# Group statistics on VectorE, the bias of v in its own rows, halved output banks, and the first image's raw weights in other tiles

## The chip, the core and the metric

The kernel runs on one core of a Trainium2 chip, on fp32 data throughout. The metric is the device time of one execution in microseconds. PE is the matmul engine, PEld its weight load, DVE the vector engine, ACT the scalar engine, POOL GpSimd, SP the engine that only issues DMAs.

## What is computed

An attention block over 16 images of 512 channels and 32 x 32 positions:

```python
xg = x.reshape(b, NUM_GROUPS, -1)                      # 8 groups of 64 channels
mu = jnp.mean(xg, axis=-1, keepdims=True)
var = jnp.var(xg, axis=-1, keepdims=True)
xn = ((xg - mu) * jax.lax.rsqrt(var + EPS)).reshape(b, c, h, w)
xn = xn * norm_gamma[:, None, None] + norm_beta[:, None, None]
qkv = jnp.einsum('oc,bchw->bohw', qkv_w, xn) + qkv_b[:, None, None]
q, k, v = jnp.split(qkv, 3, axis=1)                    # 4 heads of 128 channels
attn = jax.nn.softmax(jnp.einsum('bhnd,bhmd->bhnm', q, k) * scale, axis=-1)
out = jnp.einsum('bhnm,bhmd->bhnd', attn, v)
...
out = jnp.einsum('oc,bchw->bohw', proj_w, out) + proj_b[:, None, None]
return x + out
```

## The kernel before

Channels lie on the 128 partitions: an image is four tiles `x` of 128 x 1024 (`load_x`). The attention of an image goes head by head; a head has 8 blocks of 128 keys, and a *step* is one block. In each step, for each half of 512 queries, `scores` makes one 128x512 matmul into a bank `s` (L844), ACT takes its exp into `p` (L850), and `weighted_sum` adds the block before to the output bank `po` (L912). `po` is one tile of two banks, one half of the queries in each, with a single buffer; after the last block ACT copies each half to `o` (L919). On DVE, `tot` sums the exps (L856, L858; the additions are kept in `added[b, h, j]`), `denominators` transposes and reduces that sum, `spread_inverse` sends the reciprocals through DRAM to all partitions, and `divide` multiplies `o` (L922) four blocks into the next head.

The projections (q and k, for each pair of heads; v; the output projection `proj`) use Strassen's seven products on two levels, in `two_levels` and `strassen`. The outer level has four groups of products (`OUTER`); each makes seven inner products of 256 columns (L604) in banks `x` and `y`. ACT copies some to SBUF (`u`, L484), and DVE adds the others to results `R` in three tiles `r0`, `r1`, `r2` (L628, tag `r{g % 3}`, one buffer each). `combine` adds the groups (L677), and `finish` makes the final rows: for q and k one scalar_tensor_tensor with the bias (L712); for v an addition into a tile `vt` (L766), a transpose by 32 x 32 blocks into `vu` (L769), a DMA to DRAM (L777) and back as `v` (L782). `vt`, `vu`, the staged weights of site v and proj in the first image, and the residual `y` of the output projection share the four buffers of `ypool`.

These projection units lie between the steps. `plan_head` gives each of a head's 8 blocks a list of units: head 0 takes the second pair's q and k, head 1 the projection of the image before, head 2 the first pair's q and k of the next image, head 3 the v of the next image. Where an instruction of a unit stands on its engine is set by a scheduler at build time, by priorities (`tc.high_priority(URGENT)`) and by order edges (`tc.issue_after(ins)`: behind `ins` on its engine).

In head 1 the next image is also normalised. `stats_chunk` makes, on ACT, the mean and variance of each channel of a chunk. `stats_group` brings them together over the 64 channels of a group, in three parts that are tied to `added[b - 1, 1, n]`: `Norm.group_steps` multiplies the four columns of means by the averaging matrix `avg` on PE (`pm`, L83), takes the deviations on DVE (L82 to L87), multiplies again (`pv`, L88), adds EPS (L89), and POOL raises to the power -0.5 (L90). `scale` and `shift` make the factors (L76, L100, L102), and `normalise` applies them to halves of chunks, on ACT (L109) or, in image 0 for even chunks, on DVE (L112). `x_sums` then makes Strassen's sums of x.

The first image has more to do. There weights are loaded raw (`stage_blocks`, L355, on SP's queue), summed (`stage_sums`, L387 and L388), turned into factors (`group_weights`, L415 to L439) and kept in DRAM (L441, `kept_v`, `kept_proj`), whence later images load them (L406). `kept_group` does this for v in blocks 0 and 1 of head 1, for proj in blocks 3 to 6, after `stage_blocks("proj")` in block 2. `bias_of_v` multiplies proj's staged weights by the bias of v, one column each, on PE (`pb`, L935), and adds the product to proj's bias, so that v's bias need not be added anywhere else.

The last image's projection (`last_projection`, L999) is written out by hand. `general_path` is not taken with these inputs.

Of the kernel before, what the change touches and what calls it, by code (L numbers as in the profile page):

```python
# [10 lines left out]
F32 = mybir.dt.float32  # L11
# [175 lines left out]
def fast_path(ctx, tc, x, sources, out, consts, flag, dims):  # L187
# [35 lines left out]
    ones = one.tile([BLK, 1], F32, name="ones")  # L223
    xs, xb, vs, qs, ks, os_, ob = {}, {}, {}, {}, {}, {}, {}
# [23 lines left out]
    nc.vector.memset(neghalf, -0.5)  # L248
    for t, src in (
        (gamma_sb, gamma), (beta_sb, beta), (qkb_sb, qk_b), (vb_sb, v_b), (projb_sb, proj_b)  # L250
    ):
        nc.gpsimd.dma_start(t, src)
# [3 lines left out]
    def stats_chunk(b, c):  # L256
        if c == 0:
            mvs[b] = gn.tile([P, NCC, 2], F32, tag="mv", name=f"mv_{b}")

        junk = lpool.tile([P, N], F32, tag="tt", name=f"junk_{b}_{c}")  # L260
        sums = gn.tile([P, 3], F32, tag="st", name=f"sums_{b}_{c}")
        nc.scalar.activation(junk, xs[b, c], AF.Identity, accum_out=sums[:, 0:1])
        nc.scalar.mul(mvs[b][:, c, 0:1], sums[:, 0:1], 1.0 / N)
        nc.scalar.mul(sums[:, 1:2], sums[:, 0:1], -1.0 / N)
        nc.scalar.activation(
            junk, xs[b, c], AF.Square, bias=sums[:, 1:2], accum_out=sums[:, 2:3]
        )
        nc.scalar.mul(mvs[b][:, c, 1:2], sums[:, 2:3], 1.0 / N)

    def stats_group(b):  # L270


        g = []

        def part(n, first, last):
            if not g:
                g.extend(norm.group_steps(mvs[b]))
            with tc.issue_after(added[b - 1, 1, n].ins), tc.high_priority(URGENT):
                for step in g[first:last]:
                    step()  # L280

        def scale():
            n = 4 if b > 1 else 3
            part(n, 9, 10)
            with tc.issue_after(added[b - 1, 1, n].ins), tc.high_priority(URGENT):
                mu, sc = norm.result
                sh = norm.shift(mu, sc)
            for c in range(NCC):
                scaled[b, c] = sc, sh, c

        return [lambda: part(2, 0, 6), lambda: part(3, 6, 9), scale]
# [75 lines left out]
    def stage_blocks(site):  # L367
# [4 lines left out]
        if site in ("proj", "v"):  # L372
# [381 lines left out]
    def v_groups(b):  # L754
# [3 lines left out]
        def finish(which, h, a, c):  # L758
            pair, half = int(which[1]) - 1, int(which[2]) - 1
            if (b, pair) not in vs:  # L760
# [4 lines left out]
            t = ypool.tile([P, HALF], F32, tag="y", name=f"vt_{b}_{pair}_{h}_{half}")  # L765
            nc.vector.tensor_add(t, a, c)  # L766
# [4 lines left out]
                t.rearrange("p (j q i) -> p j q i", q=n, i=BLK),  # L771
# [135 lines left out]
    def weighted_sum(s, half):  # L907
        b, h, j = where(s)
        if j == 0 and half == 0:
            po[b, h] = ps_o.tile([P, N], F32, tag="o", name=f"po_{b}_{h}")  # L910
        i = ts(half, HALF)
        nc.tensor.matmul(  # L912
            po[b, h][:, i], v_block(b, h, j), ps[s][:, i],
            start=(j == 0), stop=(j == NB - 1),
        )
        if j == NB - 1:
            if (b, h) not in os_:
                os_[b, h] = opool.tile([P, N], F32, tag="o", name=f"o_{b}_{h}")
            last_eviction[b] = nc.scalar.copy(os_[b, h][:, i], po[b, h][:, i])  # L919

    def divide(b, h):
        nc.vector.tensor_mul(os_[b, h], os_[b, h], rinv.pop((b, h)))  # L922

# [4 lines left out]

    def bias_of_v(o):

        acc = ps_a.tile([P, HALF], F32, tag="y", name=f"pb_{o}")
        half, r = divmod(o, 2)
        for c in range(NCC):
            block = stage["proj"][f"a{half + 1}{c // KC + 1}"]
            nc.tensor.matmul(  # L935
                acc[:, 0:1], block[:, ts(r * KC + c % KC, P)], vb_sb[:, c : c + 1],
                start=(c == 0), stop=(c == NCC - 1),
            )
        nc.vector.tensor_add(
            projb_sb[:, o : o + 1], projb_sb[:, o : o + 1], acc[:, 0:1]  # L940
        )
# [116 lines left out]

    def plan_head(b, h):
# [9 lines left out]
        elif h == 1:  # L1069
# [4 lines left out]
            else:  # L1074
                plan[0].append(lambda: load_x(b + 1))
                spread(plan, [lambda c=c: stats_chunk(b + 1, c) for c in range(NCC)], 2, 4)
                sums, power, scale = stats_group(b + 1)
                if b == 0:

                    plan[4] += [sums, power, scale]  # L1080
                else:
                    plan[4].insert(0, sums)
                    plan[4].insert((len(plan[4]) + 1) // 2, power)
                    plan[5].insert(0, scale)
                for r in range(2):
                    plan[5 + r] += [

                        lambda c=c, half=half: normalise(b + 1, c, half, b > 0 or c % 2 == 1)
                        for c in range(KC * r, KC * r + KC) for half in range(NH2)
                    ]  # L1090
                plan[6].append(lambda: x_sums(b + 1, (1,)))
            if b == 0:
                for g in range(len(OUTER)):
                    plan[g // 2].append(lambda g=g: kept_group("v", g))
                    plan[NB // 2 - 1 + g].append(lambda g=g: kept_group("proj", g))
                plan[2].append(lambda: stage_blocks("proj"))
                spread(plan, [lambda o=o: bias_of_v(o) for o in range(NCC)], 3, 5)
# [111 lines left out]

    plan = []  # L1210
    for s in range(steps + 1):
# [12 lines left out]
        for half in range(NH2):  # L1224
            if s < steps:
# [4 lines left out]
                if half == 1 and j == 4 and s > NB:  # L1230

                    with tc.issue_after(added[b, h, 4].ins):
                        divide(*where(s - NB)[:2])
            if s > 0:
# [12 lines left out]
def general_path(ctx, tc, x, sources, out, consts, dims):  # L1247
# [26 lines left out]
    with tc.For_i(0, B, 1) as b:  # L1274
# [16 lines left out]
        for h in range(HEADS):  # L1291
# [9 lines left out]
            for qb in range(NB):  # L1301
# [27 lines left out]
                nc.scalar.copy(o[h][:, ts(qb, P)], acc[:, :P])  # L1329
# [46 lines left out]
```

## Time and profile before

| | |
|---|---|
| time, median of 3 runs | 3169.58 us (3167.83 to 3171.18) |
| the profiled execution | 3171.08 us, of which the span 3169.3 |
| granted TensorE clock | 1.00 throughout |
| busy: PE, DVE, ACT, POOL | 3156.8, 2635.8, 1438.3, 516.3 us |
| one image in the middle (pv to pv) | 195.8 us |
| L83 pm, 128x4, and L88 pv, 128x4 | 30 passes each, mean 214 and 263 ns |
| L935 pb, 128x1 | 32 passes, mean 245 ns |
| L766 vt, L769 vu, L712 qk (DVE) | 711, 1131, 744 ns |
| L109 normalise, L985 bias of 128x1024 (ACT) | about 0.81 and 1.14 us |

An fp32 matmul is two passes, each with its own weight load, and the profile counts passes. A line of the timeline is: start in us, length in us, engine, source line, operation, output<-inputs, shape, how many in a row, and in brackets the idle time before it and what ended it. Matmuls overlap, so the length of a pass is more than its distance to the next start. A line of the waits is: who <- waited for whom: us in total, times, longest.

### The profile page before, as it was taken

Reading aid. Unit: us, or ns where it says so; the run is one execution under the profiler, and the core shown is the slowest. Engines: PE = TensorE matmul, PEld = TensorE weight load, DVE = VectorE, ACT = ScalarE, POOL = GpSimd, SP = SyncE. Lnnn points to the kernel's source line nnn. Section 1 sums busy time; section 2 is a strip of 40 time slices with the busy share of each in tenths; the row PEclk is TensorE's granted clock in tenths of the full one; section 3 lists DMA queues with packets and bytes.
Section 4 is the critical chain, followed back from the end, with each engine's and each line's share of the span. In section 5 each row is a group of like instructions: output and inputs, shape, how many; then the busy total and the mean of one; then the engine's idle time right before and its main releaser. Section 6 shows DMA issues by size and latency. Waiting matters only on the chain.

```text
span 3169.3 us, 34227 instructions
## 1 busy us (share of the span) xinstructions
PE 3156.8 (100%) x10502; PEld 2188.2 (69%) x10502; DVE 2635.8 (83%) x4642; ACT 1438.3 (45%) x2711; POOL 516.3 (16%) x896
## 2 busy tenths in 40 slices
PE   9999999999999999999999999999999999999999
PEld 7566676677776776767767667677676776766664
DVE  9878879788897888878888787987879978788785
ACT  3535435354353443535435454453534545344333
POOL 0011221111211112211122111222012221122200
PEclk9999999999999999999999999999999999999999
DMA  5554554545545555454554545555455564555531
GB/s 176 186 190 154 187 173 152 173 152 194 168 164 163 155 184 176 167 165 144 193 173 159 170 144 192 167 174 171 144 177 170 176 187 133 178 158 187 180 119 48
DMA packets 210668, 524.83 MB, mean 166 GB/s; under 512 B 32176, under 2 KB 65456, under 8 KB 210480
## 3 DMA queue, kind: packets, MB, share of 16 engines
q1 hardware_dynamic: 133088, 282.39, 28.6%
q0 software_dynamic: 64000, 204.54, 19.3%
q10 hardware_dynamic: 13392, 35.66, 3.5%
q8 instruction: 86, 1.41, 0.2%
q14 instruction: 102, 0.84, 0.1%
HBM read 389.30 MB, written 133.17 MB: 165 GB/s over the span
## 4 chain that ended last, share of the span: by engine, by line
PE 96%; DVE 2%; DMA 1%; issue 0%; SPq 0%; POOL 0%; ACT 0%; ACTq 0%; DVEq 0%
PE s L844 27%; PE po L912 27%; PE qk_x L604 12%; PE qk_y L604 9%; PE pp_x L604 6%; PE v_x L604 6%; PE v_y L604 4%; PE pp_y L604 4%; PE lx L999 0%; DVE qk_t L572 0%; DMA x<-in_x 0%; PE ly L999 0%; DVE tot L858 0%; DVE qk_r L628 0%; DVE qk L712 0%
## 5 line engine op out<-in xcount | busy, mean ns | idle before, releaser
L912 PE MATMUL po<-p,v 128*128 128x512 f32 x2048 | 1049.4, 594 | 0.7 <-ACT p L850 0.7
L850 ACT ACTIVATE p<-s 128x512 f32<-128x512 f32 x1024 | 610.6, 596 | 963.7 <-PE s L844 960.0
L844 PE MATMUL s<-qk,qk 128*128 128x512 f32 x2048 | 1047.4, 593 | 0.3 <-DVE qk L712 0.3
L912 PEld LDWEIGHTS po<-p,v 128*128 128x128 f32 x2048 | 603.6, 302 | 322.7 <-issue 214.5
L858 DVE TENSOR_TENSOR tot<-tot,p 128x1024 f32<-128x1024 f32 x385 | 470.2, 1221 | 158.1 <-ACT p L850 156.1
L844 PEld LDWEIGHTS s<-qk,qk 128*128 128x128 f32 x2048 | 387.7, 190 | 88.6 <-issue 29.9
L604 PEld LDWEIGHTS qk_x<-qk_t,w 128*128 128x128 f32 x1344 | 251.8, 190 | 166.1 <-issue 75.3
L604 PE MATMUL qk_x<-qk_t,w 128*128 128x256 f32 x1344 | 356.3, 382 | 0.1
L484 ACT COPY qk_u<-qk_x 128x512 f32<-128x512 f32 (+1 forms) x256 | 136.2, 532 | 229.6 <-PE qk_x L604 229.6
L777 POOL DMA_DIRECT2D vd<-vu x120 | 66.6, 556 | 902.9 <-DVE vu L769 899.5
L628 DVE TENSOR_TENSOR qk_r<-qk_y,qk_u 128x512 f32<-128x512 f32 (+1 forms) x256 | 158.1, 618 | 34.7 <-ACT qk_u L484 21.5
L578 POOL DMA_DIRECT2D kept_t<-qk_t x240 | 129.3, 540 | 278.5 <-DVE qk_t L572 212.0
L604 PEld LDWEIGHTS pp_x<-pp_t,w_proj 128*128 128x128 f32 x630 | 117.2, 190 | 74.7 <-issue 32.3
L628 DVE TENSOR_TENSOR v_r<-v_y,v_u 128x512 f32<-128x512 f32 (+1 forms) x120 | 76.6, 638 | 110.5 <-ACT v_u L484 80.3
L604 PE MATMUL pp_x<-pp_t,w_proj 128*128 128x256 f32 x630 | 167.8, 383 | 0.0
L782 POOL DMA_DIRECT2D v<-vd x240 | 140.5, 592 | 166.6 <-DMA vd<-vu 63.3
L604 PE MATMUL v_x<-v_t,w_v 128*128 128x256 f32 x630 | 166.6, 381 | 0.0
L828 POOL DMA_DIRECT2D out_y<-y x120 | 65.9, 550 | 603.3 <-DVE y L827 601.5
L604 PEld LDWEIGHTS v_x<-v_t,w_v 128*128 128x128 f32 x630 | 118.4, 190 | 55.3 <-issue 19.1
L604 PE MATMUL qk_y<-x,w 128*128 128x256 f32 x512 | 142.2, 379 | 1.5 <-DVE qk_r L628 1.5
L769 DVE STREAM_TRANSPOSE vu<-vt 128x512 f32<-128x512 f32 x120 | 135.7, 1131 | 4.5 <-DMA vd<-vu 4.4
L712 DVE SCALAR_TENSOR_TENSOR qk<-qk_r,qkb_sb,qk_r 128x512 f32<-128x512 f32 x192 | 137.7, 744 | 1.6
(203 smaller groups left out, 4420.0 us busy)
## 6 DMA issues: line engine op xcount, KB each, us to landing
w<-kept SPq DMA_DIRECT2D x90, 512.0 KB, 3.7
kept_t<-qk_t POOLq DMA_DIRECT2D x180, 256.0 KB, 3.5
v_t<-kept_t SPq DMA_DIRECT2D x180, 256.0 KB, 2.9
w<-kept SPq DMA_DIRECT2D x90, 384.0 KB, 3.3
rinv<-row ACTq DMA_DIRECT2D x63, 512.0 KB, 5.0
x<-in_x POOLq DMA_DIRECT2D x60, 512.0 KB, 4.6
vd<-vu POOLq DMA_DIRECT2D x120, 256.0 KB, 3.0
v<-vd POOLq DMA_DIRECT2D x240, 128.0 KB, 4.2
```

The source lines that it names most:

```text
L484: nc.scalar.copy(t[n][:, :width], t["x"][:, :width])
L578: nc.gpsimd.dma_start(t, to)
L604: nc.tensor.matmul(acc[:, ts(i, Q)], have["w"][t][:, i, slot, :], inner(i, bn), start=(first and i == 0), stop=True, skip_group_check=True,)
L628: nc.vector.tensor_add(dst, view(a), view(c))
L712: nc.vector.scalar_tensor_tensor(st[b, h][:, ts(half, HALF)], a, qkb_sb[:, i : i + 1], c, ALU.add, ALU.add)
L769: nc.vector.transpose(u.rearrange("p (q i j) -> p j q i", q=n, i=BLK), t.rearrange("p (j q i) -> p j q i", q=n, i=BLK),)
L777: nc.gpsimd.dma_start(rows[which][ts(h, P), :], u)
L782: nc.gpsimd.dma_start(vs[b, pair][ts(q, BLK), half].rearrange("m h (k i) j -> m (h k) (i j)", k=n), rows[which].rearrange("(k m) (q e) -> ...
L844: nc.tensor.matmul(sc, ks[b, h][:, ts(j, P)], qs[b, h][:, ts(half, HALF)], start=True, stop=True)
L850: exps[s] = nc.scalar.activation(ps[s][:, ts(half, HALF)], sc, AF.Exp, scale=SCALE)
L858: added[b, h, j] = nc.vector.tensor_add(tot[b, h][:, i], tot[b, h][:, i], ps[s][:, i])
L912: nc.tensor.matmul(po[b, h][:, i], v_block(b, h, j), ps[s][:, i], start=(j == 0), stop=(j == NB - 1),)
```

## The change

The group statistics of images 1 to 15 move from PE to DVE: `stats_chunk` writes mean and sum of squares into a `table` of 128 x 2 x 32, zero but for four columns. `gather` transposes it by 32 x 32 blocks, copies each quadrant's rows to its neighbour, and aggregates 64 triples (count, mean, sum of squares) with bn_aggr; `scale` transposes the result back. It is tied to `added[b - 1, 1, 3]`, the scaling as before. `bn_aggr`'s input is in the tile of tag `tt`.

The bias of v is added in v's `finish`, in place in the tile of the result (`c`), so that `vt` goes; in image 0 it is added to `o` by ACT after the division, in blocks 2 of heads 2 and 3 and of image 1's head 0, and in block 6 of the latter. The 16 matmuls `pb` go.

`po` becomes two tiles of one bank each. In the first image proj's raw weights are staged in `r0` and `r1`, at the start of block 0 of head 1, and `kept_group("proj")` runs in blocks 2 to 5. Image 1 is normalised there one chunk at a time: the even chunks in blocks 5 and 6 on DVE, the odd ones a block later on ACT, each instruction behind an exp.

```diff
+    table = one.tile([P, 2, BLK], F32, name="table")
...
+    nc.gpsimd.memset(table, 0.0)
...
     def stats_chunk(b, c):
-        if c == 0:
-            mvs[b] = gn.tile([P, NCC, 2], F32, tag="mv", name=f"mv_{b}")
-
+        mean, spread_ = (
+            (mvs[b][:, c, 0:1], mvs[b][:, c, 1:2]) if b == 0
+            else (table[:, 0, c : c + 1], table[:, 1, c : c + 1])
+        )
...
-        nc.scalar.mul(mvs[b][:, c, 0:1], sums[:, 0:1], 1.0 / N)
+        nc.scalar.mul(mean, sums[:, 0:1], 1.0 / N)
...
-            junk, xs[b, c], AF.Square, bias=sums[:, 1:2], accum_out=sums[:, 2:3]
+            junk, xs[b, c], AF.Square, bias=sums[:, 1:2],
+            accum_out=sums[:, 2:3] if b == 0 else spread_,
         )
-        nc.scalar.mul(mvs[b][:, c, 1:2], sums[:, 2:3], 1.0 / N)
+        if b == 0:
+            nc.scalar.mul(spread_, sums[:, 2:3], 1.0 / N)
 
     def stats_group(b):
-        g = []
-
-        def part(n, first, last):
-            if not g:
-                g.extend(norm.group_steps(mvs[b]))
-            with tc.issue_after(added[b - 1, 1, n].ins), tc.high_priority(URGENT):
-                for step in g[first:last]:
-                    step()
+        v = nc.vector
+        quads = P // BLK
+        k = slice(0, NCC)
+        t = {}
+
+        def gather():
+            t["all"] = lpool.tile([P, N], F32, tag="tt", name=f"groups_{b}")
+            rows = t["all"][:, : 6 * BLK].rearrange("p (s j) -> p s j", s=3)
+            both = t["both"] = t["all"][:, 6 * BLK : 6 * BLK + 2]
+            ve = t["all"][:, 6 * BLK + 2 : 6 * BLK + 3]
+            v.memset(rows[:, 0, :], float(N))
+            v.transpose(rows[:, 1:3, :BLK], table)
+            for q in range(quads):
+                v.tensor_copy(rows[ts(q, BLK), 1:3, BLK:], rows[ts(q ^ 1, BLK), 1:3, :BLK])
+            v.bn_aggr(both, rows.rearrange("p s j -> p j s"))
+            v.tensor_scalar_add(ve, both[:, 1:2], EPS)
+            nc.gpsimd.tensor_tensor(both[:, 1:2], ve, neghalf[:, 0:1], ALU.pow)
 
         def scale():
-            n = 4 if b > 1 else 3
-            part(n, 9, 10)
-            with tc.issue_after(added[b - 1, 1, n].ins), tc.high_priority(URGENT):
-                mu, sc = norm.result
-                sh = norm.shift(mu, sc)
+            back = t["all"][:, 8 * BLK : 10 * BLK].rearrange("p (s j) -> p s j", s=2)
+            v.transpose(back, t["both"].unsqueeze(2).to_broadcast([P, 2, BLK]))
+            sc = gn.tile([P, NCC], F32, tag="sc", name="sc")
+            v.tensor_mul(sc, back[:, 1, k], gamma_sb)
+            sh = norm.shift(back[:, 0, k], sc)
...
-        return [lambda: part(2, 0, 6), lambda: part(3, 6, 9), scale]
+        def part(n, step):
+            with tc.issue_after(added[b - 1, 1, n].ins), tc.high_priority(URGENT):
+                step()
+
+        return [lambda: part(3, gather), lambda: part(4 if b > 1 else 3, scale)]
...
-        if site in ("proj", "v"):
+        if site == "proj":
+            r = [
+                rpool.tile([P, 2, 2, HALF], F32, tag=f"r{i}", name=f"st_{site}_{i}")
+                for i in range(2)
+            ]
+            for i, n in enumerate(names):
+                st[n] = r[i // 4][:, i // 2 % 2, i % 2, :]
+        elif site == "v":
...
-            t = ypool.tile([P, HALF], F32, tag="y", name=f"vt_{b}_{pair}_{h}_{half}")
-            nc.vector.tensor_add(t, a, c)
+            i = 2 * pair + h
+            nc.vector.scalar_tensor_tensor(c, a, vb_sb[:, i : i + 1], c, ALU.add, ALU.add)
...
-                t.rearrange("p (j q i) -> p j q i", q=n, i=BLK),
+                c.rearrange("p (j q i) -> p j q i", q=n, i=BLK),
...
-        if j == 0 and half == 0:
-            po[b, h] = ps_o.tile([P, N], F32, tag="o", name=f"po_{b}_{h}")
+        if j == 0:
+            po[half] = ps_o.tile([P, HALF], F32, tag=f"o{half}", name=f"po_{b}_{h}_{half}")
...
+    def bias_of_v(b, h):
+        nc.scalar.activation(os_[b, h], os_[b, h], AF.Identity, bias=vb_sb[:, h : h + 1])
...
-    def bias_of_v(o):
-        acc = ps_a.tile([P, HALF], F32, tag="y", name=f"pb_{o}")
...
+    def behind_exp(unit):
+        with tc.issue_after(exps[max(exps)].ins):
+            unit()
...
-                sums, power, scale = stats_group(b + 1)
+                gather, scale = stats_group(b + 1)
                 if b == 0:
-                    plan[4] += [sums, power, scale]
+                    plan[4] += [gather, scale]
                 else:
-                    plan[4].insert(0, sums)
-                    plan[4].insert((len(plan[4]) + 1) // 2, power)
+                    plan[4].insert(0, gather)
                     plan[5].insert(0, scale)
                 for r in range(2):
...
+                    if b > 0:
+                        plan[5 + r] += units[0] + units[1]
+                    else:
+                        plan[5 + r] += units[0]
+                        for at, u in zip((0, NB), units[1]):
+                            plan[6 + r].insert(at, lambda u=u: behind_exp(u))
...
-                    plan[NB // 2 - 1 + g].append(lambda g=g: kept_group("proj", g))
-                plan[2].append(lambda: stage_blocks("proj"))
-                spread(plan, [lambda o=o: bias_of_v(o) for o in range(NCC)], 3, 5)
+                    plan[NB // 2 - 2 + g].append(lambda g=g: kept_group("proj", g))
+                plan[0].insert(0, lambda: stage_blocks("proj"))
...
+    biased = {(h + 2) * NB + 2: h for h in range(HEADS - 1)}
+    biased[HEADS * NB + 6] = HEADS - 1
...
+                if half == 1 and s in biased:
+                    with tc.issue_after(exps[s].ins):
+                        bias_of_v(0, biased[s])
```

More of the change, by code (lines that the diff above doesn't have):

```diff
@@ L908, in weighted_sum @@
         b, h, j = where(s)
-        if j == 0 and half == 0:
-            po[b, h] = ps_o.tile([P, N], F32, tag="o", name=f"po_{b}_{h}")
+        if j == 0:
+            po[half] = ps_o.tile([P, HALF], F32, tag=f"o{half}", name=f"po_{b}_{h}_{half}")
         i = ts(half, HALF)
         nc.tensor.matmul(
-            po[b, h][:, i], v_block(b, h, j), ps[s][:, i],
+            po[half], v_block(b, h, j), ps[s][:, i],
             start=(j == 0), stop=(j == NB - 1),
@@ L918, in weighted_sum @@
                 os_[b, h] = opool.tile([P, N], F32, tag="o", name=f"o_{b}_{h}")
-            last_eviction[b] = nc.scalar.copy(os_[b, h][:, i], po[b, h][:, i])
+            last_eviction[b] = nc.scalar.copy(os_[b, h][:, i], po[half])
     def divide(b, h):
         nc.vector.tensor_mul(os_[b, h], os_[b, h], rinv.pop((b, h)))
+    def bias_of_v(b, h):
+        nc.scalar.activation(os_[b, h], os_[b, h], AF.Identity, bias=vb_sb[:, h : h + 1])
     def spread(plan, units, first, last):
@@ L927, in spread @@
             plan[first + i * (last - first) // len(units)].append(u)
-    def bias_of_v(o):
-        acc = ps_a.tile([P, HALF], F32, tag="y", name=f"pb_{o}")
[L932 to L941, printed above, removed]
     def kept_group(site, g):
@@ L1076, in plan_head @@
                 spread(plan, [lambda c=c: stats_chunk(b + 1, c) for c in range(NCC)], 2, 4)
-                sums, power, scale = stats_group(b + 1)
+                gather, scale = stats_group(b + 1)
                 if b == 0:
-                    plan[4] += [sums, power, scale]
+                    plan[4] += [gather, scale]
                 else:
-                    plan[4].insert(0, sums)
-                    plan[4].insert((len(plan[4]) + 1) // 2, power)
+                    plan[4].insert(0, gather)
                     plan[5].insert(0, scale)
                 for r in range(2):
-                    plan[5 + r] += [
-                        lambda c=c, half=half: normalise(b + 1, c, half, b > 0 or c % 2 == 1)
-                        for c in range(KC * r, KC * r + KC) for half in range(NH2)
-                    ]
+                    units = [
+                        [lambda c=c, half=half: normalise(b + 1, c, half, b > 0 or c % 2 == 1)
+                         for half in range(NH2)]
+                        for c in range(KC * r, KC * r + KC)
+                    ]
+                    if b > 0:
[4 more added lines that the diff above has]
+                            plan[6 + r].insert(at, lambda u=u: behind_exp(u))
                 plan[6].append(lambda: x_sums(b + 1, (1,)))
@@ L1328, in general_path @@
                     )
-                nc.scalar.copy(o[h][:, ts(qb, P)], acc[:, :P])
+                nc.scalar.activation(
+                    o[h][:, ts(qb, P)], acc[:, :P], AF.Identity, bias=vb_sb[:, h : h + 1]
+                )
         for i in range(NCC):
```

## The prediction

> **What bounds the kernel now.** I read the page first: busy times, then the chain that ended last. Then PE's own waits, then PE's instructions in order of time in the places that the change touches, and last the neighbours on DVE.
>
> The page:
> ```profile
> span 3169.3 us, 34227 instructions
> ...
> PE 3156.8 (100%) x10502; PEld 2188.2 (69%) x10502; DVE 2635.8 (83%) x4642; ACT 1438.3 (45%) x2711; POOL 516.3 (16%) x896
> ...
> PE 96%; DVE 2%; DMA 1%; issue 0%; SPq 0%; POOL 0%; ACT 0%; ACTq 0%; DVEq 0%
> ```
> PE carries the chain from end to end; what it does not do any more is time won, if nothing else then comes last. Since PE is "busy" also while a pass waits for its weights, I don't count busy time but the distance between starts. Undisturbed, a 512-wide pair of passes (one fp32 matmul) takes 0.86 us, four 256-wide passes 0.86, two 0.43.
>
> The waits of PE, longest first:
> ```profile
> PE qk_y L604 <- DVE qk_r L628: 1.5, 1, 1.5
> ...
> PE pm L83 <- DVE mean L82: 1.2, 1, 1.2
> PE po L912 <- ACT p L850: 0.7, 1, 0.7
> PE qk_x L604 <- DMA w<-kept: 0.6, 1, 0.6
> ```
> 6.1 us in all with the four that are left out, each once. A steady image takes 195.8 us, and PE stands still in none of it. So a gain must come from passes that go away.
>
> PE in order of time, image 6 (the statistics of image 7):
> ```profile
> 1290.04 1.03 PE L604 MATMUL pp_x<-pp_t,w_proj 128*128 128x256 f32 x4
> 1290.90 0.28 PE L83 MATMUL pm<-mean,avg 128*128 128x4 f32 x2
> 1291.04 1.11 PE L604 MATMUL pp_x<-ot,w_proj 128*128 128x256 f32 x4
> 1291.99 1.02 PE L844 MATMUL s<-qk,qk 128*128 128x512 f32 x2
> ...
> 1297.60 0.59 PE L604 MATMUL pp_y<-ot,w_proj 128*128 128x256 f32 x2
> 1298.11 0.39 PE L88 MATMUL pv<-vv,avg 128*128 128x4 f32 x2
> 1298.36 1.10 PE L844 MATMUL s<-qk,qk 128*128 128x512 f32 x2
> 1299.30 1.02 PE L912 MATMUL po<-p,v 128*128 128x512 f32 x2
> ```
> Two four-column matmuls look like nothing, and cost this: pm 0.14 to the next start, and the four passes behind it take 0.95 instead of 0.86, so 0.23. pv starts 0.51 after a pair that needs 0.43, takes 0.25, and the pair behind it takes 0.94 instead of 0.86: 0.41. Together 0.64 us an image.
>
> PE in order of time, image 0, head 1:
> ```profile
> 122.31 1.84 PE L935 MATMUL pb<-vb_sb,st_a 128*128 128x1 f32 x16
> 124.02 1.10 PE L844 MATMUL s<-qk,qk 128*128 128x512 f32 x2
> ...
> 130.11 1.02 PE L912 MATMUL po<-p,v 128*128 128x512 f32 x2
> 132.35 0.39 PE L83 MATMUL pm<-mean,avg 128*128 128x4 f32 x2 [1.22 <-DVE mean L82]
> ```
> Sixteen one-column passes take 1.71 (0.107 each) and 0.08 behind them; the other sixteen, at 134.72 and 136.56, take 0.90 and 0.81, and 0.08 behind each. Before pm, PE starts 2.24 after a pair that needs 0.86: it stood 1.38.
>
> **The change, part by part.**
>
> *Group statistics on DVE.* pm and pv go for images 1 to 15: 14 x 0.64 = 8.96; at image 0 (for image 1) pm, pv and what they push cost 0.65, and the wait of 1.38 has no matmul left to hold. 10.99 us off the path.
>
> In exchange DVE gets twelve small instructions an image for nine. Bounds by its rows: the memset 0.1 (128x4 0.06, 128x128 0.17); a transpose of 128x64 0.23 (between 0.19 for 32x32 and 1.24 for 128x1024); four copies of 32x64 at 0.19 (32x32 adds, 0.18); bn_aggr over 192 elements 0.40 (0.21 over 12, 0.69 for bn_stats over 512); the add of EPS 0.15: 1.6 us in one piece. Then a second transpose 0.23 and three of 0.15. Total 2.3 for 1.4: 0.9 more. What hides it: the piece comes behind the addition of block 3 to the total, which in image 7 ends at 1490.7; there DVE idles 1.19 us before pp_y's eviction at 1493.16, and two additions of 0.75 and 0.68 that nobody waits for can go behind that. POOL's power works on one column instead of four (1.94 us), the scale still waits for the addition of block 4, 3 us on, so the normalisation starts as before. ACT loses four 0.20 us scalings an image, off the path. POOL's new memset of the table stands ahead of the five DMAs of constants: 0.1 for the memsets that stand there, and gamma and beta land at 6.3 and some 8 us, first used at 10.5: nothing.
>
> *Bias of v.* The 32 pb passes go: 1.79 + 0.98 + 0.89 = 3.66 us off the path. The sum that made v's rows (L766, 0.711) becomes a scalar_tensor_tensor in place (L712's form, 0.744): 0.27 us an image on DVE. In image 0 ACT gets four 128x1024 passes of 1.14 (L985's form), each behind an exp. Behind it on ACT wait evictions and exps; the trace has ACT runs of 2.2 us (three normalisations) without a stop of PE. The last of the four also holds the o sums on DVE at block 6 of image 1. Nothing to 2 us; I take 0.3.
>
> *vt no longer takes a y tile.* Four y tiles serve vu instead of two. DVE stood 1.53 and 0.79 us for vd<-vu at 2984 and 2994, and the qk_y wait of 1.49 at 2998.9 is DVE late by less than that. Bounds 0 to 1.6; I take 1.2, as the 2.3 us are more than the wait.
>
> *Two po tiles of 512.* The last pass pair of a head's second half waits now for the eviction of its first half, being one tile. Where nothing else runs on PE (3083.66, 3085.58, 3111.54, 3113.46, 3138.56) a po pair takes 1.06 instead of 0.86. 5 x 0.2 = 1.0.
>
> *proj's raw weights in r0 and r1, a block earlier.* Eight loads on SP (0.4 to 1.1 us each to issue), put before those of v's raw weights, must wait for the last qk sum of pair 1 (L712 at 110.0, done 110.7); if SP is held there, v's loads and stores queue behind and are 10 us late. The kernel before issued the eight between 100.1 and 123.5, waiting for y tiles, and DVE waited 3.6 us for the last. So proj's chain should end some us earlier and w<-kept (at 159.2 PE starts 0.9 late) with it: bounds +0.9 (gone) to -3 (a longer wait instead); I take 0.2 won. r0 must be free at 156, when the first sum of qk(1,0) is evicted; st was last read at 146.4. Cover: 9.5 us.
>
> *Normalising chunk by chunk behind an exp* moves two ACT and no DVE instruction per chunk later by a block (3.4 us): x's sums follow, and qk(1,0) was ready only by 153.9 against x at 142.4. 0 to 2 us; I take 0.2.
>
> *The tight place.* This is where the DVE additions meet PE, at each image's head 0:
> ```profile
> 1428.63 0.69 DVE L317 TENSOR_TENSOR ot<-ot,o 128x512 f32<-128x512 f32 x1
> 1429.24 0.68 DVE L628 TENSOR_TENSOR qk_r<-qk_y,qk_u 128x512 f32<-128x512 f32 x1
> ```
> DVE is busy 35.8 of the 36 us from 1395 to 1431 (v's transposes), this eviction ends at 1429.92, and PE's next pass into the same bank starts at 1430.12: 0.2 us of cover, against 0.27 us added ahead of it. 0 to 1.0 an image; nearest is 0.1, so 14 x 0.1 = 1.4 lost.
>
> **Sum**, against the profiled run (3171.08, of which 3169.3 is the span): -10.99 - 3.66 - 1.2 - 1.0 - 0.2 + 0.3 + 0.2 + 1.4 = -15.15, so 3155.9. That run lies 1.50 above the median of 3169.58; on the median's scale 3154.4.
>
> **Rivals.**
> *A, DVE becomes the bound.* The 0.9 + 0.27 us an image land on PE. For: 83% busy, saturated for 36 us around head 0. Against: nothing stops PE there today, and 0.9 of it falls in head 1, where DVE idles. If 1.0 of it lands each image: 3154.4 + 14 x 0.9 = 3167.
>
> *B, slower: v's result tile is held longer.* The sum is now written into the r tile, which is free only after its transpose (1.13) and no longer after the addition; qk's first eviction of the next image needs r0. If the two transposes of c12 come between the bank and that eviction, the tight place is late by 2 x 1.13 + 0.27 - 0.2 = 2.3 us, 14 times: 32 us lost for 16.5 won, 3185. It turns slower from 1.6 us an image on. Against: the last vu transposes run at 1425.5, ahead of the eviction at 1429.24, already; the order of work there would have to change.
>
> *C, PE does not give the time back.* What holds the passes behind pm, pv and pb may be something else that is late there. Then only the distance between pm's own two passes comes back for each (together 0.28, one 0.25: 0.03): 92 x 0.03 = 2.8, with the wait of 1.4 and some 2 of the other waits 6.2: 3163. Against: the 0.107 between pb's passes recurs sixteen times in a row, and four passes take 0.95 for 0.86 behind pm alone. [...]
>
> *D, the first image gets worse:* SP held for r0, v's weights and proj's late together, 5 us at the start of head 2; still 3160.
>
> **Numbers.** Forecast 0.80 (its own range 3150 to 3161), A 0.08, B 0.05, C 0.03, D 0.04. What a measurement can tell from no change is about 0.2%, 6.3 us. Faster takes the forecast, D and a quarter of A: 0.86. Same: the rest of A and C, 0.09. Slower: B, 0.05. Lowest: all three waits gone and no cost at the tight place, 3150; highest, with most of A and C inside, 3166.
>
> **What would show it.** Right: pm, pv, pb gone from PE in images 0 to 14, a steady image 0.5 to 0.7 us shorter (195.1 to 195.3), no DVE wait on vd<-vu, no qk_y wait of 1.5 near the end. Wrong: a PE wait on DVE qk_r or v_r in every image (A, B), a steady image of 195.8 or more, or a wait of PE on w<-kept over 3 us at 150 to 170 (D).

## The result, and the profile after

The change makes the kernel slower: 3179.84 us, median of 7 runs (3177.96 to 3182.65), against 3168.61 for the kernel before (3167.81 to 3171.18, 7 runs); ratio 1.0034, 95% interval 1.0023 to 1.0046. The profiled execution took 3177.96 us (span 3176.2), 6.9 more than that of before. The medians are 11.2 apart: the profiled execution of after is the fastest of its seven, that of before lies 2.5 above its median. The forecast was 15 less.

The page after, in the lines that answer to those shown of before (span; busy time and instructions; the chain that ended last):

```profile
span 3176.2 us, 34096 instructions
...
PE 3153.0 (99%) x10410; PEld 2175.0 (68%) x10410; DVE 2666.9 (84%) x4683; ACT 1438.2 (45%) x2655; POOL 495.4 (16%) x897
...
PE 87%; DVE 10%; issue 2%; DMA 1%; ACT 0%; ACTq 0%; DVEq 0%; POOL 0%; SPq 0%; POOLq 0%
```

PE has the 92 passes less that were to go (10502 to 10410), yet the chain now runs through DVE for 10% of the span instead of 2%. The waits of PE (who, for whom: us in total, times, longest) say where:

```profile
PE v_y L629 <- DVE v_r L653: 10.3, 30, 0.4
PE qk_x L629 <- DVE l L898: 2.4, 1, 2.4
...
PE s L869 <- ACT p L875: 1.1, 1, 1.1
```

The waits on pm and on qk_r near the end are gone, as forecast. The 2.4 before qk_x, put down to `l`, is a wait for w<-kept: that load landed at 152.28, just as `l` ended, and PE started at 152.42. New is a wait of v_y on the eviction v_r, thirty times: twice in head 3 of each of the first fifteen images. (An eviction is the DVE instruction that takes finished products out of a bank, so that PE may write there again.) I take the length of an image from head 0's TENSOR_REDUCE on DVE to that of the next image. Between images 2 and 13 it was 195.79 us and is 196.65 (means). With 0.63 of pm and pv gone, 1.5 has come in. PE in order of time, in head 3 of image 6, which makes the v of image 7, and at the end of head 1 of image 7:

```profile
1403.83 1.04 PE L937 MATMUL po<-p,v 128*128 128x512 f32 x2
1405.13 1.13 PE L629 MATMUL v_y<-xt,w_v 128*128 128x256 f32 x4 [0.26 <-DVE v_r L653]
1406.10 0.59 PE L629 MATMUL v_x<-x,w_v 128*128 128x256 f32 x2
...
1412.98 1.03 PE L937 MATMUL po<-p,v 128*128 128x512 f32 x2
1414.45 0.70 PE L629 MATMUL v_y<-x,w_v 128*128 128x256 f32 x2 [0.43 <-DVE v_r L653]
1414.98 1.02 PE L869 MATMUL s<-qk,qk 128*128 128x512 f32 x2
...
1514.78 1.04 PE L937 MATMUL po<-p,v 128*128 128x512 f32 x2
1515.85 0.70 PE L629 MATMUL pp_y<-o,w_proj 128*128 128x256 f32 x2
1516.39 1.02 PE L869 MATMUL s<-qk,qk 128*128 128x512 f32 x2
```

A po pair needs 0.86 to the next start. The first v_y starts 1.30 after it, 0.44 late, and its four passes take 0.97 for 0.86: 0.55 lost (**first wait**). The second starts 0.61 late and its two passes take 0.10 too long, which they also did before: 0.61 new (**second wait**). The pp_y at the end of head 1 starts 0.21 late and loses 0.11: 0.32 (**third wait**, with 0.07 more a block earlier); the waits view does not list it, because PE counts as busy until 1515.82. The same places on DVE:

```profile
1402.08 1.27 DVE L883 TENSOR_TENSOR tot<-tot,p 128x1024 f32<-128x1024 f32 x1
1403.21 1.27 DVE L947 TENSOR_TENSOR o<-o,rinv 128x1024 f32<-128x1024 f32 x1
1404.34 0.74 DVE L653 TENSOR_TENSOR v_r<-v_y,v_u 128x512 f32<-128x512 f32 x1
...
1409.81 1.44 DVE L791 SCALAR_TENSOR_TENSOR v_r<-v_r,vb_sb,v_r 128x512 f32<-128x512 f32 x2
1411.13 2.08 DVE L794 STREAM_TRANSPOSE vu<-v_r 128x512 f32<-128x512 f32 x2
1413.01 0.73 DVE L791 SCALAR_TENSOR_TENSOR v_r<-v_r,vb_sb 128x512 f32<-128x512 f32 x1
1413.61 0.46 DVE L653 TENSOR_TENSOR v_r<-v_y,v_p 128x256 f32<-128x256 f32 x1
1413.94 0.46 DVE L653 TENSOR_TENSOR v_r<-v_y,v_u 128x256 f32<-128x256 f32 x1
```

The same stretch of head 3 on DVE in the kernel before:

```profile
1400.80 1.27 DVE L858 TENSOR_TENSOR tot<-tot,p 128x1024 f32<-128x1024 f32 x1
1401.92 0.75 DVE L628 TENSOR_TENSOR v_r<-v_y,v_u 128x512 f32<-128x512 f32 x1
1402.52 1.28 DVE L922 TENSOR_TENSOR o<-o,rinv 128x1024 f32<-128x1024 f32 x1
...
1408.80 1.17 DVE L769 STREAM_TRANSPOSE vu<-vt 128x512 f32<-128x512 f32 x1
1409.74 0.74 DVE L766 TENSOR_TENSOR vt<-v_r,v_r 128x512 f32<-128x512 f32 x1
...
1410.66 0.48 DVE L628 TENSOR_TENSOR v_r<-v_y,v_p 128x256 f32<-128x256 f32 x1
1410.99 0.48 DVE L628 TENSOR_TENSOR v_r<-v_y,v_u 128x256 f32<-128x256 f32 x1
1411.32 1.14 DVE L769 STREAM_TRANSPOSE vu<-vt 128x512 f32<-128x512 f32 x1
```

First wait: the division of o (L947) now stands ahead of the eviction; before, it stood behind it. Second wait: two transposes in a row and three additions of v stand ahead of the two evictions; before, it was one transpose and two additions (the first at 1407.86), with the second transpose behind the evictions. PE's own order of matmuls has not changed here.

At the third wait, too, DVE's order has changed. The addition to the total stands ahead of the eviction in the kernel after (shown first), and behind it in the kernel before:

```profile
1514.25 1.22 DVE L883 TENSOR_TENSOR tot<-tot,p 128x1024 f32<-128x1024 f32 x1
1515.38 0.41 DVE L653 TENSOR_TENSOR pp_r<-pp_y,pp_u 128x256 f32<-128x256 f32 x1
```

```profile
1511.81 0.42 DVE L628 TENSOR_TENSOR pp_r<-pp_y,pp_u 128x256 f32<-128x256 f32 x1
...
1512.74 1.22 DVE L858 TENSOR_TENSOR tot<-tot,p 128x1024 f32<-128x1024 f32 x1
```

The profiled 6.9 us add up by stages: the first 112 us -0.2, image 0 -1.3 (182.91 to 181.63), the next image +0.1, twelve images of +0.86 together +10.4, the last period -0.9 (the qk_y wait of 1.5 gone, head 3's two waits new), the tail behind it -1.2. Of this, 0.82 is the po pairs: from head 0's reduction in the last image to the last reduction of all it takes 103.98 in the two kernels with one po tile (before and e14, below), and 103.15 to 103.38 in all others.

The steady images repeat from run to run: e10, e12, e15 and e16, which differ in the first image alone, have 195.35 to 195.38. The first image does not: e1 and e8 run the same instructions there, and it took 182.94 and 181.06 in their profiles. So differences of up to 2 us in it, in single profiles, are not yet effects, and neither is image 0's -1.3.

### The profile page after: what moved, and what is told of

Read it like the earlier page. It is cut to its first block, busy times and chain, and to the rows that moved or that the text cites. A ratio compares the mean times of both kernels' runs of the same rounds, so it can differ in the third digit from the quotient of the medians.

```text
span 3176.2 us, 34096 instructions
## 1 busy us (share of the span) xinstructions
PE 3153.0 (99%) x10410; PEld 2175.0 (68%) x10410; DVE 2666.9 (84%) x4683; ACT 1438.2 (45%) x2655; POOL 495.4 (16%) x897
## 4 chain that ended last, share of the span: by engine, by line
PE 87%; DVE 10%; issue 2%; DMA 1%; ACT 0%; ACTq 0%; DVEq 0%; POOL 0%; SPq 0%; POOLq 0%
PE s L869 24%; PE po L937 24%; PE qk_x L629 12%; PE qk_y L629 9%; PE pp_x L629 6%; PE pp_y L629 4%; PE v_x L629 4%; PE v_y L629 3%; DVE vu L794 2%; DVE v_r L653 1%; DVE qk_t L597 1%; DVE v_r L702 1%; DVE tot L883 1%; DVE v_r L791 1%; DVE o L947 1%
## 5 line engine op out<-in xcount | busy, mean ns | idle before, releaser
L509 ACT COPY v_u<-v_x 128x512 f32<-128x512 f32 (+1 forms) x124 | 66.2, 534 | 156.1 <-PE v_x L629 129.4
```

The source lines that it names most:

```text
L509: nc.scalar.copy(t[n][:, :width], t["x"][:, :width])
```

## Experiments

The steady image is the mean from images 2 to 13 as above; the kernel before ran beside every group at 3168.5 to 3169.0.

| run | median us | ratio to before (95%) | steady image |
|---|---|---|---|
| after | 3179.84 | 1.0034 (1.0023 to 1.0046) | 196.65 |
| e1_vt | 3165.76 | 0.9989 (0.9980 to 0.9998) | 195.68 |
| e2_nobias | 3177.25 | 1.0023 (1.0014 to 1.0033) | 196.47 |
| e3_pestat | 3181.43 | 1.0040 (1.0026 to 1.0053) | 196.90 |
| e4_first | 3181.88 | 1.0041 (1.0027 to 1.0055) | 196.64 |
| e5_swap22 | 3178.01 | 1.0028 (1.0017 to 1.0039) | 196.54 |
| e6_swap | 3180.04 | 1.0034 (1.0022 to 1.0046) | 196.64 |
| e7_vt_half | 3159.76 | 0.9971 (0.9960 to 0.9982) | 195.29 |
| e8_vt_sums_later | 3165.56 | 0.9990 (0.9981 to 0.9999) | 195.67 |
| e9_dead_rows | 3172.70 | 1.0009 (1.0000 to 1.0018) | 196.14 |
| e10_vt_two_aggr | 3161.97 | 0.9977 (0.9967 to 0.9987) | 195.36 |
| e11_vt_stores_pool | 3165.41 | 0.9988 (0.9979 to 0.9997) | 195.70 |
| e12_all | 3161.52 | 0.9976 (0.9966 to 0.9986) | 195.38 |
| e13_tail_later | 3169.55 | 1.0000 (0.9991 to 1.0009) | 195.88 |
| e14_before_in_place | 3182.50 | 1.0042 (1.0028 to 1.0056) | 196.71 |
| e15_two_aggr_old_stage | 3162.50 | 0.9981 (0.9972 to 0.9990) | 195.38 |
| e16_two_aggr_old_norm | 3161.75 | 0.9978 (0.9969 to 0.9987) | 195.35 |

### The sum of v in place: e1, e2, e14

```diff
# e1: the kernel after, with
-            nc.vector.scalar_tensor_tensor(c, a, vb_sb[:, i : i + 1], c, ALU.add, ALU.add)
+            t = ypool.tile([P, HALF], F32, tag="y", name=f"vt_{b}_{pair}_{h}_{half}")
+            nc.vector.scalar_tensor_tensor(t, a, vb_sb[:, i : i + 1], c, ALU.add, ALU.add)
...
-                c.rearrange("p (j q i) -> p j q i", q=n, i=BLK),
+                t.rearrange("p (j q i) -> p j q i", q=n, i=BLK),
# e2: the kernel after, with
-            nc.vector.scalar_tensor_tensor(c, a, vb_sb[:, i : i + 1], c, ALU.add, ALU.add)
+            nc.vector.tensor_add(c, a, c)
# e14: the kernel before, with
-            t = ypool.tile([P, HALF], F32, tag="y", name=f"vt_{b}_{pair}_{h}_{half}")
+            t = c
```

> The kernel after, but v's finish writes its sum (with the bias, scalar_tensor_tensor) into a tile vt of ypool again instead of in place into the result tile, and the transpose reads vt. Theory T1 (the result tile, held until its transpose, and the order on DVE that follows from it, make PE wait twice in each image's head 3): both waits of PE v_y on DVE v_r at 1405 and 1414 of the kernel after go, the v_r waits of PE fall from 10.3 us to under 2, a steady image takes 195.5 instead of 196.65 us, and the time is about 15 us under the kernel after: 3162 to 3166. Rival R1 (the costlier sum with the bias, 0.03 us an instruction, or DVE being full there, is what holds PE): the waits stay, 3178 to 3181. The qk_y wait near the end of 1.5 may come back, vt being in the four y buffers again.

> The kernel after, but v's sum in images 1 to 15 is a plain tensor_add, still in place; v's bias is left out there. T1: the waits stay, 3177 to 3180, since the tile is held as long. Rival R1 (the bias in the sum is what costs): the waits go, 3162 to 3166.

> The kernel before with one part of the change alone: v's sum (still a plain addition, v's bias still in proj's bias) goes in place into the result tile instead of into vt. T1: both waits of head 3 appear by that alone, 1.0 to 1.1 us an image, 15 of them: a steady image 196.8, 3183 to 3186. Rival R1e (it takes the bias sum or the other parts as well): under 196.2 and 3175.

e1 came out 14 us under the kernel after, and the v_y wait is in its waits no more. The evictions stand again where they stood before, with the second transpose behind them (DVE of e1):

```profile
1408.09 1.14 DVE L795 STREAM_TRANSPOSE vu<-vt 128x512 f32<-128x512 f32 x1
...
1409.96 0.45 DVE L653 TENSOR_TENSOR v_r<-v_y,v_p 128x256 f32<-128x256 f32 x1
1410.30 0.45 DVE L653 TENSOR_TENSOR v_r<-v_y,v_u 128x256 f32<-128x256 f32 x1
1410.63 1.12 DVE L795 STREAM_TRANSPOSE vu<-vt 128x512 f32<-128x512 f32 x1
```

e14 is the proof from the other side: in the kernel before, this one edit brings both waits and costs 13.6 us, 0.92 an image in 15 images. The waits of PE in e14:

```profile
PE v_y L604 <- DVE v_r L628: 7.4, 30, 0.3
```

e2, which leaves v's bias out of images 1 to 15, gives the rest: an image is 0.18 shorter, so the rival holds for that much. 0.92 + 0.18 = 1.10 an image, 16.5 us in 15 images, is what this part of the change costs in head 3. The other way round, e1 wins back 0.97 and is still 0.13 late at the second place (v_y starts 1.00 behind its po pair, for 0.87 before).

On the qk_y wait near the end the runs say two things. In e14 it is gone by this edit alone (the last period is 196.70, as the other images), and DVE waits for vd<-vu nowhere. But e1 does not bring it back, and neither does any other run with vt in y tiles: in e1 DVE waits for vd<-vu three times, 0.45 to 0.83 us, at no place where it costs PE time. So it is open whether the y tiles earned those 1.5 us or the one profile of the kernel before had a late store there.

### Held tile or order: e5, e6, e9, e13

```diff
# e5: the kernel after, with, for v only
-                done("c22", (2, 0), (0, 1))
-                done("c21", (2, 0), (2, 1))
+                done("c21", (2, 0), (2, 1))
+                done("c22", (0, 1), (2, 0))
# e6: e5, and for v only
-                done("c11", (0, 0), (1, 0))
-                add((1, 1), (0, 0), (1, 1))
+                add((1, 1), (0, 0), (1, 1))
+                done("c11", (1, 0), (0, 0))
# e9: the c11 of e6, c22 ahead of c21 as in the kernel after, but its sum written into (1, 1)
# e13: e9, each transpose of c22 and c21 (with its DMAs) made one unit later
+            waiting.append(tail)
+            while len(waiting) > (1 if which in ("c22", "c21") else 0):
+                waiting.pop(0)()
```

> The kernel after, v's sums still in place with the bias, but c22 after c21 and written into (2,0), a row of r2, instead of (0,1), a row of r0. Theory T1a: of the two waits of PE on v_r in head 3 the second (0.59 us, before v_y at 1414.45) comes from r0: group 3's results share it, and its first write waits for c22's two transposes. So that wait goes and the first (0.53, at 1405.13) stays: a steady image 196.1, 8.9 us under the kernel after, 3170 to 3172. Rival R1a (DVE has simply too much to do there, whoever holds which tile): both waits stay, 3178 to 3181.

> As the one before, and c11 is written in place into (0,0) instead of (1,0), after the addition that still reads (0,0). T1b: the first wait (0.53, at 1405.13) comes from the addition into (1,0), which in the kernel after overwrites c11's result and so must come behind its two transposes; that bunches them ahead of the eviction. Both waits go, as with a tile vt, with no tile of ypool: a steady image 195.6 to 195.7, 15 to 17 us under the kernel after, 3162 to 3166. Rival R1b (the first wait comes from the order of the division and the eviction alone, whatever (1,0) holds): as the kernel before this one, 3170 to 3172.

> The kernel after, with no tile vt, but v's sums written into rows that nobody reads any more: c11 into (0,0) behind the addition that reads it, c22 into (1,1) of r1, in the order of the kernel after (c22 before c21). In e5 and e6 c22 stood behind c21, so that r0 came free only with c22's late additions; here it comes free with c22's early additions, no transpose between. T1c: the second wait in head 3 (0.59) was r0 held by whatever reads or fills its row (0,1) last. Both waits go, as in e1: v_r waits of PE under 2 us in all, a steady image 195.6 to 195.8, 3163 to 3167. Rival R1c (a tile of its own in ypool is what matters, any write into a result tile disturbs): a v_r wait of 0.5 or more stays in each image, 3173 to 3181.

> The kernel e9 (v's sums in dead rows), with each transpose of c22 and c21 and its DMAs made one place later in the order of the units. Theory T1d: what is left of the second wait in e9 (0.59 us before v_y) is the order on DVE alone: without a tile of ypool for the sum, the transposes no longer wait for a buffer and stand ahead of, and between, the two evictions that PE waits for. Here an addition of 0.72 stands between the evictions where e9 has a transpose of 1.08: the wait is 0.36 shorter, a steady image 195.8 instead of 196.14, 5 us under e9, 3167 to 3169. Rival R1d (what holds the evictions is a result tile, not the order): 196.1 and 3172 to 3174 again.

Here c11 to c22 are the quarters of v, and (g, i) is result i of outer group g, in tile `r{g % 3}`: group 3 writes into r0 again.

e5 and e6 missed on the second wait. In e5 it stayed (v_y 0.46 late), in e6 it grew to 1.07: c22's sums, which read r0, now stood behind c21's, and the evictions into r0 behind them (1416.45 in e6). So the edit had changed two things at once. The first wait did go in e6, and again in e9: with c11 written into (0,0) the eviction stands ahead of the division. Why the order at build time turns on that row is not shown.

In e9 no transpose reads r0 at the second place any more, and the second wait stayed at 0.61. So the held tile, my theory and the mechanism of rival B, is not needed for it. (In the kernel after, the tile does hold the evictions behind both transposes of c22; e9 has the wait without that.) DVE of e9:

```profile
1410.34 1.42 DVE L799 SCALAR_TENSOR_TENSOR v_r<-v_r,vb_sb,v_r 128x512 f32<-128x512 f32 x2
1411.66 1.13 DVE L802 STREAM_TRANSPOSE vu<-v_r 128x512 f32<-128x512 f32 x1
1412.61 0.43 DVE L653 TENSOR_TENSOR v_r<-v_y,v_p 128x256 f32<-128x256 f32 x1
1412.94 1.08 DVE L802 STREAM_TRANSPOSE vu<-v_r 128x512 f32<-128x512 f32 x1
1413.88 0.40 DVE L653 TENSOR_TENSOR v_r<-v_y,v_u 128x256 f32<-128x256 f32 x1
```

A transpose stands between the two evictions that PE needs. e13 puts an addition there instead:

```profile
1410.56 0.43 DVE L653 TENSOR_TENSOR v_r<-v_y,v_p 128x256 f32<-128x256 f32 x1
1410.89 0.74 DVE L799 SCALAR_TENSOR_TENSOR v_r<-v_r,vb_sb 128x512 f32<-128x512 f32 x1
1411.53 0.43 DVE L653 TENSOR_TENSOR v_r<-v_y,v_u 128x256 f32<-128x256 f32 x1
```

From v_p to v_u it is 0.97 instead of 1.27, and a steady image is 0.26 shorter (0.36 was expected), though e13 holds the result tiles longer, as the transposes that read them come later. So the order of transposes, additions and evictions on DVE makes that part of the second wait. v_y is still 0.34 late in e13; there the addition stands between the two evictions, which are 0.33 apart in the kernel before. No run takes that out by itself. In the kernel before and in e1, two tiles of ypool for each piece pace the transposes, so that they fall behind the evictions; that this is why is argued from the buffers, while the order itself is shown.

### The statistics on DVE: e3, e7, e8, e10

```diff
# e3: the kernel after with stats_chunk, stats_group and their places as in the kernel before
# e7: e1, with half of each group left out of the statistics
-            for q in range(quads):
-                v.tensor_copy(rows[ts(q, BLK), 1:3, BLK:], rows[ts(q ^ 1, BLK), 1:3, :BLK])
-            v.bn_aggr(both, rows.rearrange("p s j -> p j s"))
+            v.bn_aggr(both, rows[:, :, :BLK].rearrange("p s j -> p j s"))
# e8: e1, with
-                plan[6].append(lambda: x_sums(b + 1, (1,)))
+                plan[6 if b == 0 else 7].append(lambda: x_sums(b + 1, (1,)))
# e10: e1, with rows, pair_ and both in tiles of their own, the counts set once, and
+            v.transpose(rows[:, 1:3, :], table)
+            v.bn_aggr(pair_[:, 0, 1:3], rows.rearrange("p s j -> p j s"))
+            for q in range(quads):
+                v.tensor_copy(pair_[ts(q, BLK), 1, 1:3], pair_[ts(q ^ 1, BLK), 0, 1:3])
+            v.bn_aggr(both, pair_)
```

> The kernel after, with the group statistics on PE as in the kernel before (pm, pv and their DVE steps for all images). Theory T2 (gather and scale on DVE make PE wait at the end of head 1, 0.38 us in each of 14 images, against 0.64 of PE that they save): those waits go (-5.3), pm and pv come back (+9.0), and the wait before pm in image 0 (+1.4): about 5 us over the kernel after, 3183 to 3186; a steady image 196.9. Rival R2 (the statistics on DVE cost as much as they save, and more, because DVE is late behind them in other places too): no slower than the kernel after, 3174 to 3180.

> The kernel e1 (v's sum in a tile vt), but gather makes no copies and aggregates 32 triples instead of 64: the statistics then cover half of the channels of a group. Theory T2 (the wait of PE before pp_y at the end of head 1, 0.31 with 0.07 beside it, is DVE late by the length of gather): the four copies (0.78) and about half of bn_aggr (1.01, estimate 0.5) go, 1.3 us in all, more than the wait, so it is gone: a steady image 195.3, 5 us under e1, 3159 to 3162; bn_aggr over 96 elements takes 0.5 to 0.6. Rival R2a (the wait comes from scale's new transpose and the order behind it): a steady image stays at 195.7, 3164 to 3167.

> The kernel e1, but the sums of x for the next image (two additions of 0.68 on DVE) are planned in block 7 of head 1 instead of block 6, for images 2 to 15. T2: that takes 0.68 off DVE ahead of the late eviction before pp_y, and the wait of 0.31 with 0.07 beside it goes: a steady image 195.3, 5 us under e1, 3159 to 3162. Rival R2b (the additions go only where DVE was idle anyway, or qk of head 2 then waits for them): 3164 to 3168.

> The kernel e1 with a shorter gather that computes the same: bn_aggr over each quadrant's 32 triples (96 elements, 0.57 in e7), four copies of 32x2, bn_aggr over the two pairs (6 elements), the counts set once. By rows: 0.19 + 0.57 + four copies at about 0.15 + 0.2 = 1.5 instead of 2.1 (0.11 + 0.19 + 0.78 + 1.01). T2: DVE is late before pp_y by less than that, so the wait of 0.31 with 0.07 beside it goes: a steady image 195.3, 3159 to 3162. Rival R2c (the 0.6 is not enough, or falls into idle time of DVE): 195.5 to 195.7, 3163 to 3166.

The groups of the kernel after show what gather is made of:

```profile
L292 DVE BATCH_NORM_AGGREGATE groups<-groups 128x2 f32<-128x192 f32 x15 | 15.2, 1015 | 0.0
L291 DVE COPY groups<-groups 32x64 f32<-32x64 f32 x60 | 11.1, 186 | 0.8
...
L288 DVE MEMSET groups<- 128x64 f32 x15 | 1.7, 112 | 0.0
```

and those of e10:

```profile
L292 DVE COPY pair<-pair 32x2 f32<-32x2 f32 x60 | 9.6, 160 | 1.1
L290 DVE BATCH_NORM_AGGREGATE pair<-rows 128x2 f32<-128x96 f32 x15 | 8.7, 577 | 0.0
...
L293 DVE BATCH_NORM_AGGREGATE both<-pair 128x2 f32<-128x6 f32 x15 | 2.6, 175 | 0.0
```

e7 and e10 both lose the third wait: the pp_y passes follow the po pair at once, and a steady image is 0.39 and 0.32 under e1, 6.0 and 3.8 us in all. So a shorter gather is enough to end it, and e10 computes the same in some 0.5 us less. What e10 saves is bn_aggr (0.26 of the 1.01) and the memset (0.11); its four copies of two columns take almost as long as those of 64 (0.160 for 0.186). The addition to the total stands ahead of the eviction in e1, e7 and e10 alike, and behind it in e3: that order is a part of the wait that no run changes by itself. e8 failed: only one of the two additions moved (1512.67 in e1), and that one stood behind the late eviction (1511.74) already. e3's steady image came as expected, 0.25 above the kernel after, since the statistics earn 0.63 and lose 0.38; its time is only 1.6 above by the medians and 3.1 by the profiles, not 5: image 0 has no wait for p of 1.1 there, and only 0.5 before pm instead of 1.4, which I had not counted.

### The first image: e4, e11, e12, e15, e16

```diff
# e4: the kernel after, with (e15: the same staging on e10; e16: the same normalising on e10)
-        if site == "proj":
-            r = [
...
-        elif site == "v":
+        if site in ("proj", "v"):
...
-                        for at, u in zip((0, NB), units[1]):
-                            plan[6 + r].insert(at, lambda u=u: behind_exp(u))
+                    plan[5 + r] += units[0] + units[1]
...
-                    plan[NB // 2 - 2 + g].append(lambda g=g: kept_group("proj", g))
-                plan[0].insert(0, lambda: stage_blocks("proj"))
+                    plan[NB // 2 - 1 + g].append(lambda g=g: kept_group("proj", g))
+                plan[2].append(lambda: stage_blocks("proj"))
# e11: e1, with (e12: e10, with)
-            nc.sync.dma_start(store[site, g, t], w[t][:, :n])
+            eng = nc.gpsimd if site == "proj" else nc.sync
+            eng.dma_start(store[site, g, t], w[t][:, :n])
```

> The kernel after, with the first image as before: proj's raw weights staged in the tiles of ypool and ot from block 2 on, kept_group one block later, image 1 normalised as before. Theory T3 (the new places cost PE 2.4 us before qk_x on w<-kept and 1.1 us before s on ACT's p, and save some 0.8 of the old wait): 1 to 3 us under the kernel after, 3176 to 3178. Rival R3 (the early staging earns more than it costs): 1 to 3 us over it, 3181 to 3182.

> The kernel e1 with the stores of proj's factors in the first image (kept_proj) issued by POOL instead of SP. Theory T3a: the wait of 2.4 to 3.2 before the first qk_x of head 2 in image 0 is w<-kept, whose loads stand on SP behind the last kept_proj stores, which wait for DVE's last sum at 147.1; without them SP issues w<-kept some 2 us earlier, the wait falls under 1.5 us, and the passes behind it that took twice as long after the longer stops (0.21 each) run at full speed: 2 to 4 us under e1, 3162 to 3164. Rival R3a (the loads wait for the buffers that these stores free, or DVE's qk_t is as late): 3164 to 3167.

> e1, e10 and e11 together, as a version that computes the whole reference: if T2 and T3a hold, 5 and 2 to 4 us under e1, 3156 to 3160, so 0.3 to 0.4% under the kernel before; if only one does, 3160 to 3164.

> The kernel e10 with proj's raw weights of the first image staged as in the kernel before (tiles of ypool and ot, from block 2, kept_group one block later); the normalising stays as in the kernel after. Theory T3b: the new staging is what leaves PE waiting for w<-kept at the start of head 2 of image 0 (3.9 us in e10, with 1.6 lost behind it in slow passes; 0.6 in the kernel before): 3 to 5 us under e10, 3157 to 3159. Rival R3b (the old staging delays DVE's factors and the statistics behind them by as much): 3161 to 3165.

> The kernel e10 with the first image's normalising as in the kernel before (all halves of a chunk on ACT at its place, not behind an exp); the staging stays as in the kernel after. Theory T3c: in e4 the normalising stood on ACT 4.75 us for sh, ahead of the exps, and PE stood 3.3 us for p: that comes from the old normalising, so it comes back here: 2 to 5 us over e10, 3164 to 3167. Rival R3c (it came from the old staging, which held the statistics back on DVE): 3160 to 3163.

T3 fell. With the old staging and normalising, image 0 is 2.8 longer in the profiles (184.47 for 181.63); the medians are 2.0 apart, and the runs of the two overlap. PE waits 3.1 for p instead of 1.1 and 0.8 less for w<-kept, and some 1.7 is a lower clock behind the wait of 3.1 (last section). The raw weights land late, DVE's factors and the statistics behind them slip, `sh` comes at 138.3 instead of 134.7, and ACT stands for it with the exps queued behind (ACT of e4):

```profile
138.50 1.52 ACT L109 ACTIVATE x<-x,sh,sc 128x512 f32<-128x512 f32 x2 [4.75 <-DVE sh L102]
139.92 0.57 ACT L868 ACTIVATE p<-s 128x512 f32<-128x512 f32 x1
```

e15 and e16 show which of the two does it: with the old staging alone PE waits 3.0 us for p, with the old normalising alone the waits list none, as in e10. T3b and T3c both fell. So the new staging keeps the statistics early and pays with a longer wait for w<-kept (2.4 in the kernel after, 3.1 in e1, 3.9 in e10, 0.6 before). Net the times do not tell it from the old: e15 is 0.5 above e10, within the spread of both. Issuing the stores on POOL cut that wait to 2.0 in e11 but brought a new one of 1.2 on ACT's o; e11 and e12 are no faster than e1 and e10 by more than half a microsecond, so T3a fell too. The best versions that compute all of the reference are e12, e16 and e10, level at 3161.5 to 3162.0: 0.22 to 0.24% under the kernel before, beside which they ran.

## Why the prediction was wrong, point by point

- **pm, pv, pb** (-10.99, -3.66): right for pm and pv; no run brings pb back alone, so its 3.66 is not measured. All 92 passes are gone. In e7, which has them gone and the first and third wait away, a steady image is 0.50 under before's, with 0.13 still late at the second place: 0.63 for the 0.64 forecast. That is 0.16 a pass, so rival C does not agree with these runs.
- **qk_y near the end, po tiles** (-1.2, -1.0): right in size (the wait of 1.5 is gone, the po pairs earn 0.82). The reason for the first, the y tiles, is open: e14 speaks for it, e1 against it.
- **The tight place** (+1.4): the step that failed. I looked for v's in-place sum at one place, the qk eviction of head 0, because DVE was full there, and priced the 0.03 us that each sum grows by. There nothing happened. The cost lies in head 3, where an edit that takes no time changed the order on DVE: 1.10 an image, 16.5 us (e14 for 0.92 of it, e2 for 0.18). Rival B named the right edit and a longer hold of the result tile, but at the wrong place, with 0.05; e9 and e13 show the wait without the hold, by order.
- **Gather "hidden" in 1.19 us of idle time**: wrong. bn_aggr was taken at 0.40 (bounds 0.21 to 0.69) and took 1.01, so the piece is 2.2 and not 1.6 us. The idle time of 1.19 before pp_y's eviction was used up, the addition to the total came ahead of the eviction, and DVE ended head 1 late: 0.38 an image, some 5.3 us. That is rival A's kind of loss, at less than half its size.
- **The first image** (-0.2, +0.3, +0.2): w<-kept costs 1.7 more instead of 0.2 less, and the wait for p on ACT 1.2 where I had 0.2; together some 3 us, inside rival D's price, if not by its mechanism. Of the page's waits, three and not four were left out of the lines shown; their sum of 6.1 is right.
- With 16.5 + 5.3 + 3 for the terms that I had at 1.7, the sum -15.15 would have read +8; the profiled difference is +6.9, that of the medians +11.2. The 4.3 between these two are not traced.

## What to carry to other kernels

Where the order on an engine is made at build time, a change that removes a buffer or writes in place is not free because it adds no work (in e14 it cost 0.92 us an image): look at which instructions it lets run earlier, and what they then stand ahead of in a queue that PE waits on. On an engine as busy as DVE here (84% of the span in the kernel after), price each new instruction by the size that it really has, and take idle time as cover only once for all that is moved there.

## What the runs showed of the hardware

bn_aggr's time grew with its elements: 175 ns over 6 and 577 over 96 (e10), 209 over 12 (the kernel before), 1015 over 192 (the kernel after), so by estimate from these about 4.5 ns each beside some 150 ns. An fp32 addition of 512 columns took 0.68 us (L317 of the kernel before).

A long stop of PE cost more than itself in e1: PE stood 3.08 us before the first qk_x of head 2, and its next eight passes took 0.43 each instead of 0.216. The windows view of e1, with the granted clock in the third column from the end:

```profile
151.00:154.06 3.06, 0.00 (x1) 0.03 (x1) 2.98 (x10) 0.00 (x0) 0.54 (x1) 1.00 0.98 345
154.06:157.47 3.41, 3.41 (x8) 2.71 (x9) 1.28 (x3) 1.08 (x2) 0.54 (x1) 0.52 1.03 399
157.47:161.00 3.53, 3.53 (x17) 3.12 (x16) 3.21 (x8) 1.34 (x3) 0.00 (x0) 0.98 0.36 115
```

A granted clock of 0.52 for 3.41 us, 1.7 us lost. It was also down behind the stop of 3.1 in e4 (0.64 from 140.5 to 145.0), and 1.6 us were lost in slow passes behind that of 3.9 in e10. It stayed at 1.00 behind the 2.39 in the kernel after (152.4 to 156.0) and the 3.09 in e12 (151.6 to 155.0). So stops of 3.08 and 3.09 us were followed by different clocks: the length of the stop alone does not decide, and what does is not shown. By estimate the 1.7 us are most of the 1.9 us by which image 0 differs between e1 and e8.
